# Two queues in turns begin the four copies of v in self-attention

## The chip, the cores and the metric

The kernel runs on one core of a Trainium2 chip. The metric is the device time of one launch in microseconds, and what counts is the median of several runs. All data are float32. The engines are named as the profile names them: PE multiplies matrices (PEld is its weight load), DVE and ACT work on vectors and scalars, POOL is the third vector engine. SP computes nothing; its queue begins DMA transfers and waits for what they need. ACT's queue can begin transfers too, between its own computing instructions.

## What is computed

The reference is one decoder layer on x of shape 2 x 1024 x 256, in three parts, each closed by a residual sum and a layer normalisation. Only the first part is touched:

```python
q, k, v = split_heads(x @ Wq), split_heads(x @ Wk), split_heads(x @ Wv)   # 16 heads of 64
q, k = apply_rope(q), apply_rope(k)
sim = einsum('bid,bjd->bij', q, k) * scale          # causal
attn = softmax(sim)
out = einsum('bij,bjd->bid', attn, v) @ Wo + bo
```

After it come cross-attention to 77 context rows and a feed-forward block that only the better half of the tokens, chosen by a router, goes through.

## The kernel before

Self-attention is done for 16 pairs of heads: 8 pairs for each of the two batch entries, numbered 0 to 15. A pair goes through named steps, and one list of steps per period (`steps`, L487), with an opening (L526) and an ending (L539) written out by hand, puts the steps of several pairs into one order. That order is the order of instructions on every engine's queue: nothing is reordered later, and each queue takes its instructions one after the other. An instruction that has to wait holds up all that stand behind it on its own queue, and nothing on the others.

The steps that matter here, with their letters in the lists:

- `P`, `E`: PE projects x to k, q and v (L268, L303); ACT copies the results out of PSUM (L276, L312).
- `d`: SP begins two transfers that swap neighbouring rows of k and q, `turned<-raw`. `s` and `a`: POOL multiplies them by the sine table (L291) and adds them (L295), which finishes the rotary embedding. Both are done for two halves of the tokens, numbered 0 and 1.
- `S`: PE makes scores (L342). `T`: DVE masks them and finds the least (L355). `X`: ACT takes exponentials (L363). `R`: DVE transposes them within blocks of 32 by 32 into `p_t` (L372).
- `w`: SP writes v to a buffer in device memory, `v_d<-v`. `l`: the four copies `v<-v_d`, the subject of this change. DVE's transposes leave each group of 32 keys on its own quarter of the 128 partitions, and the output matmuls may multiply any quarter with any group of keys; so each quarter needs all of v: 512 KB in each of four copies, every one of them to 32 partitions.
- `V`: PE multiplies v with the exponentials (L410), eight steps V0 to V7. The first four matmuls of V0 each read another quarter. `O`: ACT copies the four results out (L422); in the last pair DVE does it (L428).
- `D`, `B`, `M`: the sums' reciprocals go to memory and come back spread along partitions (`inv_d`, `over`), and POOL scales the output by them (L431). `W`: SP stores the output, `attn_d<-out_pair`.
- `A`, `C`, `Y`, `Z` close a tile of 128 tokens of the first batch entry: SP loads the outputs of all its pairs (`attnT<-attn_d`), PE projects them (L473), the rest normalises. `f`, `F`, `g`, `z` do so for the second.

There is one v4 buffer. The copies for a pair may therefore begin only when V7 of the pair before has ended, and they must have landed before V0 of their own pair. In the lists `l` stands behind the first `O` steps of the pair before. Those wait for the end of V7 on ACT anyway, so that ACT hardly waits once more when it comes to the copies.

On SP's queue each period has, in this order: `d0`, `B`, `w`, `d1`, `D`, the three weight loads of `L`, `W`, `A`. In the ending the order differs: around the copies of pair 15 the list reads `14O3 5C 15R10 15l 15X21 13M 15T30 ... 14O1 13W 15S4 14Q ... 6A 6C`. There `13W` (attn_d) and `6A` (attnT for tile 6) stand behind `15l` in the list but on another queue, and PE runs `6C` before `15V0`. In that place `1=` stands for a few matmuls that nobody reads.

## Time and profile before

| what | value |
|---|---|
| median of 3 runs | 831.27 us (830.59 to 837.27) |
| profiled execution | 842.25 us |
| its span, first to last instruction | 840.5 us |
| granted PE clock, mean | 0.985 |
| ACT queue, all 64 copies of v, issue time | 309 / 443 / 1402 ns min / median / max |

The profile is of one execution. A line of the timeline gives the start, the busy time, engine, source line, operation, what is written and read, the count, and in brackets how long the engine had been idle and what ended that. `SPq` and `ACTq` are the queues that begin transfers; the duration of such a line is the time of issuing, not of moving the data. A transfer's landing is told separately, as the time from issue until its completion is seen. A line of sums over a window gives the stretch, its length, the busy time and count of PE, PEld, DVE, ACT and POOL, the granted clock, the mean busy share of the 16 DMA engines, and GB/s. Pair numbers are not in the profile; they come from counting the copies.

### The profile page before, as it was taken

What the parts mean: (1) busy time and instruction counts of PE and PEld (TensorE: products, weight loads), DVE (VectorE), ACT (ScalarE), POOL (GpSimd) and SP (SyncE); (2) the same over time, 40 slices, a digit from 0 to 9 for tenths busy, and PEclk for the clock granted to TensorE, in tenths of its full rate; (3) what the DMA queues carried; (4) which work ended last, traced back from release to release, by engine and by line L of the source; (5) the groups of instructions that cost most, each with busy time, mean ns of one, the idle gap of its engine ahead of it and who ended that gap; (6) DMA issues with size and microseconds to landing.
All of it is one profiled execution on the core that took longest, in us unless ns stands there. A gap on an engine that the chain in (4) does not pass through costs nothing.

```text
span 840.5 us, 26580 instructions
## 1 busy us (share of the span) xinstructions
PE 796.4 (95%) x11432; PEld 629.2 (75%) x11432; DVE 581.4 (69%) x1345; ACT 356.6 (42%) x842; POOL 367.6 (44%) x261
## 2 busy tenths in 40 slices
PE   8999999999999899999999989899999999998996
PEld 4566688888788787788787867589778888876655
DVE  2558679668668568668776796535477788876673
ACT  2545455556456455554544554200443332333220
POOL 2733554555454554463661653213032222261574
PEclk9999999999999999999999999899999999999999
DMA  5445387577468467567474585564360000011131
GB/s 176 140 135 138 117 216 181 180 197 195 128 168 205 149 187 184 172 170 183 161 195 130 150 208 161 130 188 151 132 210 1 1 1 0 1 51 51 51 101 50
DMA packets 65328, 112.32 MB, mean 134 GB/s; under 512 B 6497, under 2 KB 43707, under 8 KB 65211
## 3 DMA queue, kind: packets, MB, share of 16 engines
q1 hardware_dynamic: 54459, 72.87, 26.9%
q10 hardware_dynamic: 9216, 33.56, 18.6%
q0 software_dynamic: 1536, 4.20, 1.3%
q8 instruction: 90, 1.47, 0.8%
q14 instruction: 27, 0.22, 0.1%
HBM read 71.24 MB, written 22.59 MB: 112 GB/s over the span
## 4 chain that ended last, share of the span: by engine, by line
PE 79%; DVE 10%; issue 4%; POOL 4%; DMA 1%; ACT 1%; POOLq 0%; SPq 0%; DVEq 0%; ACTq 0%
PE po_self L410 17%; PE ps_scores L342 16%; PE pp_kq L268 13%; PE pp_v L303 7%; PE po_proj L473 5%; PE ps_cross L945 5%; PE po_cross L997 4%; DVE reach L800 2%; PE pp_h L888 2%; PE po_ffn L899 2%; DVE pT L372 2%; PE unread L244 1%; PE pt_p L977 1%; POOL e L966 1%; POOL comp L830 1%
## 5 line engine op out<-in xcount | busy, mean ns | idle before, releaser
L355 DVE CUSTOM_DVE_ANT_0 p<-ps_scores,fence 128x512 f32<-128x512 f32 (+7 forms) x256 | 179.7, 751 | 127.2 <-PE ps_scores L342 126.8
L363 ACT ACTIVATE p<-p,neg 128x768 f32<-128x768 f32 (+7 forms) x256 | 196.3, 768 | 162.5 <-DVE neg L355 160.6
L410 PE MATMUL po_self<-pT,v 32*64 32x256 f32 (+6 forms) x7808 | 160.4, 298 | 22.3 <-issue 17.5
L372 DVE STREAM_TRANSPOSE pT<-p 128x768 f32<-128x768 f32 (+7 forms) x256 | 175.8, 740 | 3.4 <-ACT p L363 1.8
L410 PEld LDWEIGHTS po_self<-pT,v 32*64 32x64 f32 x7808 | 139.1, 133 | 47.6 <-issue 36.3
L342 PE MATMUL ps_scores<-kq 64*128 64x256 f32 (+3 forms) x1056 | 151.8, 420 | 2.9 <-issue 1.3
L342 PEld LDWEIGHTS ps_scores<-kq 64*128 64x128 f32 x1056 | 95.0, 191 | 45.2 <-issue 29.8
L291 POOL TENSOR_TENSOR turned<-turned,sin 128x1024 f32<-128x1024 f32 x31 | 73.1, 2360 | 109.7 <-DMA turned<-raw 105.0
L268 PE MATMUL pp_kq<-xT,w_pair 128*128 128x256 f32 (+2 forms) x516 | 118.8, 382 | 1.3 <-ACT xT L203 0.8
L288 POOL TENSOR_TENSOR kq<-raw,cos 128x1024 f32<-128x1024 f32 x31 | 73.3, 2363 | 103.8 <-ACT raw L276 103.8
L268 PEld LDWEIGHTS pp_kq<-xT,w_pair 128*128 128x128 f32 x516 | 87.1, 191 | 25.2 <-issue 11.3
L966 POOL TENSOR_TENSOR e<-e,inv 128x616 f32<-128x616 f32 x32 | 38.2, 1215 | 113.8 <-DVE inv L965 96.1
L120 POOL TENSOR_TENSOR rs<-ve,neg_half 128x1 f32<-128x1 f32 x48 | 27.6, 577 | 113.3 <-DVE ve L118 112.1
L295 POOL TENSOR_TENSOR kq<-kq,turned 128x1024 f32<-128x1024 f32 x31 | 73.4, 2369 | 1.4
L997 PE MATMUL po_cross<-packed,pT 128*128 128x256 f32 (+1 forms) x320 | 72.5, 381 | 0.0
L945 PE MATMUL ps_cross<-wqk,x1T 128*128 128x308 f32 x256 | 69.2, 423 | 0.0
L997 PEld LDWEIGHTS po_cross<-packed,pT 128*128 128x128 f32 (+1 forms) x320 | 60.7, 192 | 8.9
L303 PEld LDWEIGHTS pp_v<-w_pair,xT 128*128 128x128 f32 x512 | 61.1, 192 | 4.0 <-issue 2.2
L303 PE MATMUL pp_v<-w_pair,xT 128*128 128x128 f32 x512 | 62.2, 275 | 0.0
L945 PEld LDWEIGHTS ps_cross<-wqk,x1T 128*128 128x128 f32 x256 | 47.4, 190 | 16.2 <-issue 0.7
L958 ACT ACTIVATE e<-e 128x616 f32<-128x616 f32 x32 | 22.9, 717 | 83.0 <-DVE e L954 83.0
L473 PE MATMUL po_proj<-wo,attnT 128*128 128x256 f32 x224 | 51.6, 381 | 1.5 <-ACT out_pair L422 1.0
(128 smaller groups left out, 830.7 us busy)
## 6 DMA issues: line engine op xcount, KB each, us to landing
v<-v_d ACTq DMA_DIRECT2D x64, 512.0 KB, 8.4
turned<-raw SPq DMA_DIRECT2D x64, 256.0 KB, 4.5
v_d<-v SPq DMA_DIRECT2D x16, 512.0 KB, 4.6
over<-inv_d SPq DMA_DIRECT2D x32, 256.0 KB, 4.7
attn_d<-out_pair SPq DMA_DIRECT2D x14, 512.0 KB, 3.8
attnT<-attn_d SPq DMA_DIRECT2D x8, 512.0 KB, 5.4
vo_d<-vo SPq DMA_DIRECT2D x2, 1232.0 KB
attnT<-attn_d SPq DMA_DIRECT2D x3, 768.0 KB, 6.5
```

The lines of the kernel that those rows point to most:

```text
L268: TE.matmul(pp[:, cols], self.w[:, c, "kq".index(of), :], x_ts[self.b, n][:, c, cols], start=(c == 0), stop=(c == NC - 1),)
L288: E.tensor_tensor(self.kq[:, :, n * NB : (n + 1) * NB], self.raw[n], self.twice(cos, n), ALU.mult)
L295: E.tensor_tensor(dst, dst, self.turned[n], ALU.add)
L303: TE.matmul(pv[:, i, :], x_ts[self.b, 2 * n // NT][:, c, toks], self.w[:, c, 2, :], start=(c == 0), stop=(c == NC - 1),)
L342: TE.matmul(self.ps[j][:, cols], self.kq[rows, 1, t * P : (t + 1) * P], self.kq[rows, 0, cols.start - at : cols.stop - at], start=True, st ...
L355: V.tensor_tensor_reduce(p[:, span], self.ps[j][:, span], fence[:, T - (t + 1) * P :], -SCALE, -MASKED, ALU.add, ALU.min, neg[:, i : i + 1],)
L363: A.activation(p[:, span], p[:, span], AF.Exp, bias=neg[:, i : i + 1], scale=-1.0, accum_out=self.sums[:, j, t : t + 1],)
L372: V.transpose(p_t[:, first : first + t * step + 1 : step, :], self.p[g, j][:, span].rearrange("p (n k) -> p n k", k=P),)
L410: ins = TE.matmul(self.po[r][j * D : (j + 1) * D, n:, :], self.v4[rows, NT * k + n, j * D : (j + 1) * D], p_t[rows, first:last:step, k * R ...
L473: TE.matmul(self.po, of, wo[:, c, :], start=(c == 0), stop=(c == NP - 1))
L945: TE.matmul(ps[:, g, : Q * S], self.x_t[:, c, :], wqk[:, c, self.b, h : h + Q, :].rearrange("p h s -> p (h s)"), start=(c == 0), stop=(c = ...
L997: TE.matmul(po, self.p_t[:w, k, :], packed[self.b][:w, k, :], start=(k == 0), stop=(k == NK - 1))
```

## The change

In step `l` the four copies are no longer all begun by ACT: quarters 0 and 2 stay on ACT's queue, quarters 1 and 3 go to SP's. Sizes, sources, destinations and the place in the lists stay.

```diff
                 self.v4 = s1.tile([P, K4, P], F32, tag="v4", name="v4")
                 for r in range(4):
-                    nc.scalar.dma_start(
+                    (nc.scalar, nc.sync)[r % 2].dma_start(
                         self.v4[r * R32 : (r + 1) * R32, :, :].rearrange("k (c n) d -> k c (n d)", c=4),
                         self.v_d.rearrange("c k e -> k c e"),
                     )
```

In the built program ACT has 32 copies fewer and SP 32 more; PE, DVE and POOL keep their instructions in the same order. On SP the two copies of a pair stand right behind the store of the next pair's v (`v_d<-v`), and for pairs 1 to 15 the first of them waits for PE. In most pairs the next transfer behind them is `turned<-raw`. In pair 14 it is `attn_d<-out_pair`; in pair 15 `over<-inv_d` stands ahead of them, and behind them come `attn_d<-out_pair` and two loads `attnT<-attn_d`.

## The prediction

> **What bounds the kernel now.** I read the page first: busy times, the chain that ended last, the table of DMA issues. Then, for the stage the change touches (self-attention, about 57 to 554 us), the timeline of every engine, sums over windows, and the landing times of single transfers.

> ```profile
> span 840.5 us, 26580 instructions
> PE 796.4 (95%) x11432; PEld 629.2 (75%) x11432; DVE 581.4 (69%) x1345; ACT 356.6 (42%) x842; POOL 367.6 (44%) x261
> PE 79%; DVE 10%; issue 4%; POOL 4%; DMA 1%; ACT 1%; POOLq 0%; SPq 0%; DVEq 0%; ACTq 0%
> v<-v_d ACTq DMA_DIRECT2D x64, 512.0 KB, 8.4
> turned<-raw SPq DMA_DIRECT2D x64, 256.0 KB, 4.5
> ```

> PE is the bound: 95% busy, 79% of the chain. The 64 copies are 4 for each of 16 pairs of heads. DMA holds 1% of the chain and ACT 1%, so a cheaper issue or an earlier landing pays only where PE waits for it. Two places decide: an ordinary pair, and the last one.

> An ordinary pair (number 3; POOL, SP and PE of the timeline, then two window sums, whose last two columns are the DMA share and GB/s):

> ```profile
> 139.76 1.13 SPq L219 DMA_DIRECT2D turned<-raw  x2
> 148.72 2.36 POOL L291 TENSOR_TENSOR turned<-turned,sin 128x1024 f32<-128x1024 f32 x1 [4.24 <-DMA turned<-raw]
> 151.16 2.38 POOL L295 TENSOR_TENSOR kq<-kq,turned 128x1024 f32<-128x1024 f32 x1
> 153.79 0.49 PE L342 MATMUL ps_scores<-kq 64*128 64x256 f32 x2
> ...
> 133.00:145.00 12.00, 12.00 (x176) 10.73 (x158) 10.63 (x17) 7.53 (x15) 4.81 (x3) 1.00 0.84 178
> 145.00:149.00 4.00, 4.00 (x29) 3.62 (x30) 2.10 (x2) 1.71 (x5) 0.28 (x1) 1.00 1.03 330
> ```

> ACT issues the four copies from 134.24 to 136.32. The last lands 11.8 us after its issue, at 147.6, and the first matmul that reads them starts at 150.36: 2.8 us to spare. The turned halves that SP issues at 139.76 land only at 148.0. The sine step waits for them, the sum ends at 153.54, and the scores start at 153.79 with PE never idle. So what stands close to PE is turned, not v, with 0.25 us of slack here.

> The last pair (15; SP, ACT, then PE):

> ```profile
> 515.18 0.33 SPq L219 DMA_DIRECT2D attn_d<-out_pair  x1
> 515.55 3.61 SPq L219 DMA_DIRECT2D attnT<-attn_d  x2
> ...
> 519.36 3.78 ACTq L322 DMA_DIRECT2D v<-v_d  x4
> 523.25 0.94 ACT L363 ACTIVATE p<-p,neg 128x768 f32<-128x768 f32 x1 [3.73 <-DVE neg L355]
> ...
> 527.55 3.72 PE L473 MATMUL po_proj<-wo,attnT 128*128 128x256 f32 x16 [0.96 <-ACT out_pair L422]
> 533.03 0.81 PE L410 MATMUL po_self<-pT,v 32*64 32x256 f32 x4
> 535.44 0.61 PE L410 MATMUL po_self<-pT,v 32*64 32x256 f32 x2 [1.60 <-DMA v<-v_d]
> 537.52 1.08 PE L410 MATMUL po_self<-pT,v 32*64 32x256 f32 x9 [1.47 <-DVE x L121]
> ```

> Here PE does wait for v: quarters 2 and 3 land at 535.3 and 537.4, and the matmuls start at 535.44 and 537.52. (The second wait is put down to DVE, but the landing is 0.1 us before it.) SP has already sent this stage's other transfers, at 515.18 and 515.55, before ACT begins.

> **The change, part by part.**

> *ACT loses two of four issues.* 64 issues take 32.1 us of ACT's queue, so 32 of them give back 16 us, 1 us a pair. ACT waits 160.6 us for DVE's minima alone, which covers it: in ordinary pairs the next exponential starts when DVE releases it. Where PE waits for ACT's copies out of PSUM the trace shows 0.48 us (492.14) and 0.96 us (527.55). I take 0.2 us of gain; the bounds are 0 and 0.5, since the second wait is replaced below.

> *SP gains two issues, about 0.5 us each, and a wait.* They stand behind the store of v and wait for the last matmul that reads the old v4 (the end of V7). Queued behind are the next turned halves, inv_d, the weights, attn_d and attnT. In pairs 1 to 13 SP is idle after that store until the turned halves, whose source comes 4 us or more after V7's end (134.1, then 139.76): cost nothing. The cover is that gap; without it each pair would pay up to 1 us on turned. Pair 0 waits for no matmul. In pair 14 the row of attn_d is issued at 489.75 and V7 ends at 489.94: nothing.

> *Do the copies land earlier?* They begin at most 0.15 us earlier (SP need not finish ACT's copy out of PSUM first). The four move 2.1 MB; a window wholly inside, 522 to 533, moved 208 GB/s with the DMA share at 1.00. [...] If the limit were the queue, the near row would be 330 GB/s (145 to 149) and the copies 10.1 - 6.4 = 3.7 us shorter. I take 0: DMA already shows a share of 1.00 on one queue's copies. Even 3.7 us is worth nothing in ordinary pairs, where PE doesn't wait.

> *Do the turned halves land later, now behind two copies on their own queue?* [...] behind SP's own copies they would land at 148, 2 us later, and with 0.25 to 2.4 us of slack in pairs 2 to 9 PE would pay 8.3 us in all (1.17, 1.75, 1.41, 1.0, 0, 1.58, 0, 1.42). The row disagrees: they already land at 148.0, after the last copy at 147.6. They already queue behind all four copies, whichever queue those use. I take 0, with 8.3 at the far end.

> *The last pair changes order.* This is the one term that isn't hidden. In the built program SP's two copies of pair 15 stand ahead of attn_d and attnT, and must wait for V7 of pair 14, which ends at 519.12. So attnT is issued not at 515.55 but after two copies and attn_d, at about 520.6, and its data go out behind the copies on the same queue. The matmuls at 527.55 (L473) need it, and PE takes them before pair 15's output. When does it land? Pair 14 shows nearly the same heap in another order: attn_d issued at 489.75, four copies, the turned halves (0.52 MB), attnT landing at 506.9, 17.15 us in all. Without the turned halves (0.52 MB at 330 GB/s, 1.6 us) it is 15.55 us from 519.2: 534.7. Then PE: L473 starts 7.15 us later; from it to the first output matmul was 533.03 - 527.55 = 5.48 us, so output starts at 540.2. By then v has long landed (519.2 + 13.4 = 532.6, as from 134.24 to 147.6). Before, output really ran from 537.52 with 6 matmuls done (0.2 us), as if from 537.3. Loss: 2.9 us. Everything from there to 600 is PE back to back (its idle sums to about 1 us), so it reaches the end.

> Sum: 2.9 - 0.2 = 2.7 us on the profiled 842.25 (span 840.5 and 1.75 around it), 844.95. That execution is 1.3% above the median of the runs, so 831.27 x 844.95 / 842.25 = 833.9 us.

> **The rivals.**

> *A: the last pair gains.* If only SP's own two copies go ahead of attn_d and attnT, and ACT's two share the rest of the time, then from 520.3 it is 1.05 MB at 209 GB/s (5.0 us) and 1.05 MB at 330 (3.2 us): attnT lands at 528.5, output starts at 534.0, 3.3 us sooner, and with ACT's 0.2 us the time is 827.8. For it: v's late landing costs PE 3.7 us now. Against it: the turned halves of pair 3, which queue behind all four copies.

> *B: slower, by the turned halves.* One mechanism: two copies ahead of them on SP's queue make them 2 us later in every pair; it decides as soon as the delay exceeds 0.25 us. 8.3 + 2.7 = 11 us: 842.2. [...] Against it: 148.0 after 147.6.

> *C: it does nothing.* The order on SP costs nothing since attnT and v trade places evenly: 831.3.

> **How the numbers follow.** Forecast 0.6 (832 to 836.5), A 0.15 (827 to 830), B 0.13 (837 to 845), C 0.12 (830 to 832). The range 829.5 to 839 leaves out about half of A and over half of B, and some scatter of the runs (830.59 to 837.27). What a measurement of this kernel tells from no change is about 1%, 8.3 us: only B's upper part is beyond it. Faster 0.02, same 0.87, slower 0.11.

> **What the profile after would show.** Ordinary pairs: ACT's copies x2 a pair, turned landing within 0.5 us of 8.2 after issue, scores without PE idle before them. Last pair: attn_d at 520 rather than 515.18; before L473 a wait of 6 to 8 us for attnT; output running without waits for v. Wrong if PE idles before L342 in most pairs (B), or if L473 near 527 isn't late (A).

## The result, and the profile after

The changed kernel takes 841.63 us (median of 17 runs, 836.6 to 849.09) against 837.1 us for the kernel before (17 runs beside them, 830.59 to 844.79). The ratio is 1.0071, interval 1.0049 to 1.0093: about 5.9 us slower (4.1 to 7.8); the two medians differ by 4.5 us. The forecast was 833.9 us in a range that ended at 839.0; direction and place were right, the size was not. The ratios leave out runs more than 1.5% above the fastest of their kernel, and as every kernel here scatters by about as much, the medians of all runs are given beside a ratio where the two differ.

Two things went wrong. The base: 831.27 us was the median of three runs; 17 runs of the same kernel, those three among them, have a median of 837.1, and 59, 36 and 54 others 837.45, 838.51 and 837.04. And the effect: 5.9 us instead of 2.7.

The two profiled executions hide all that: 842.25 us before, 841.96 after (its span is in the page), because PE reached the end of V7 of pair 14 at 519.12 before and at 513.45 after. That stretch scatters by some 9 us from run to run (511.5 to 520.2 in the fourteen traces of this study), with no instruction on PE changed. From V7's end on, the traces can be compared.

The page after (first the span; then the shares of the chain that ended last; then DMA issues, with the median from issue to landing):

```profile
span 840.2 us, 26598 instructions
PE 80%; DVE 8%; issue 4%; POOL 4%; DMA 3%; ACT 1%; SPq 0%; POOLq 0%; DVEq 0%; ACTq 0%
turned<-raw SPq DMA_DIRECT2D x64, 256.0 KB, 4.2
v<-v_d ACTq DMA_DIRECT2D x32, 512.0 KB, 7.7
v<-v_d SPq DMA_DIRECT2D x32, 512.0 KB, 10.4
```

DMA's share of the chain went from 1% to 3%. The turned halves land no later than before (median 4.2 us, before 4.5). That they land 2 us later in each pair was an estimate of rival B, which no trace showed.

Ordinary pair 3 of the kernel after, from the timeline:

```profile
140.63 1.14 SPq L219 DMA_DIRECT2D turned<-raw  x2
149.07 2.35 POOL L291 TENSOR_TENSOR turned<-turned,sin 128x1024 f32<-128x1024 f32 x1 [3.73 <-DMA turned<-raw]
151.49 2.39 POOL L295 TENSOR_TENSOR kq<-kq,turned 128x1024 f32<-128x1024 f32 x1
154.78 1.68 PE L342 MATMUL ps_scores<-kq 64*128 64x256 f32 x14
```

A stretch of the window sums of the same kernel in which only copies of v move (DMA share and GB/s last):

```profile
138.00:140.50 2.50, 2.50 (x24) 2.41 (x22) 2.50 (x5) 2.50 (x5) 0.00 (x0) 1.00 1.03 210
```

The turned halves land at 148.3, 7.7 us after their issue (before 8.2), and the scores' line carries no idle time. Copies alone move 210 GB/s; the same window of the kernel before (137.0 to 139.7) has 211. So in this pair two queues in turns neither speed the copies up nor delay what follows.

The last pair after (timeline; SP and ACT's queue, then PE):

```profile
513.48 1.73 SPq L322 DMA_DIRECT2D v<-v_d  x2
513.65 1.57 ACTq L322 DMA_DIRECT2D v<-v_d  x2
515.31 0.39 SPq L219 DMA_DIRECT2D attn_d<-out_pair  x1
515.74 11.44 SPq L219 DMA_DIRECT2D attnT<-attn_d  x2
528.25 6.14 PE L473 MATMUL po_proj<-wo,attnT 128*128 128x256 f32 x16 [7.31 <-DMA attnT<-attn_d]
536.14 6.55 PE L410 MATMUL po_self<-pT,v 32*64 32x256 f32 x268
543.56 1.79 PE L410 MATMUL po_self<-pT,v 32*64 32x128 f32 x116 [0.87 <-issue]
```

The order on SP is the one forecast: copies, then attn_d, then attnT. What the waiting copies hold up is seen in it: POOL had finished attn_d's source at 509.81, and SP issued attn_d 5.50 us later (before, 0.02 us later: 515.16 and 515.18). From 509.81 to V7's end PE, on its own queue, was busy for 3.30 of 3.64 us. (The line of 11.44 us joins two loads: the one for tile 6 is begun at 515.74, the other belongs to the second batch entry, waits for attn_d, and is begun at 526.81.) PE waits 7.31 us for attnT, and the output then runs 268 matmuls without a wait for v. One number was not forecast: the 16 matmuls of L473 take 6.14 us, and took 3.72 before. The window sums say why. They are cut at V7's end, L473, the first output matmul and the last projections, and the granted clock is the first of the last three columns. First the kernel before:

```profile
519.12:527.55 8.43, 7.47 (x33) 4.35 (x33) 8.43 (x15) 4.69 (x12) 0.00 (x0) 1.00 0.98 233
527.55:533.03 5.48, 5.48 (x21) 3.73 (x22) 5.48 (x8) 3.30 (x7) 0.00 (x0) 1.00 0.97 193
533.03:554.35 21.32, 17.41 (x509) 14.10 (x508) 5.19 (x15) 0.69 (x2) 5.62 (x6) 0.84 0.52 148
```

The same sums of the kernel after:

```profile
513.45:528.25 14.80, 7.49 (x35) 4.40 (x34) 14.49 (x22) 7.63 (x17) 0.00 (x0) 0.82 0.89 216
528.25:536.14 7.89, 7.89 (x21) 5.44 (x21) 0.75 (x1) 0.37 (x1) 0.00 (x0) 0.69 0.68 203
536.14:551.86 15.72, 13.80 (x510) 12.37 (x509) 5.90 (x14) 0.69 (x2) 5.63 (x6) 1.00 0.46 139
```

During the wait PE's granted clock fell to half (from 522.96, for 10.24 us), and it stayed there into the work behind the wait: 0.69 over the second stretch. The kernel before lost clock too, but in its third stretch (0.84): its half clock began at 536.2, behind the first and in the second of its two waits for v, and lasted 6.83 us.

### The profile page after: what moved, and what is told of

It is laid out like the page before. It is cut to its first block, busy times and chain, and to the rows that moved or that the text cites. A ratio compares the mean times of both kernels' runs of the same rounds, so it can differ in the third digit from the quotient of the medians.

```text
span 840.2 us, 26598 instructions
## 1 busy us (share of the span) xinstructions
PE 794.4 (95%) x11432; PEld 628.0 (75%) x11432; DVE 581.1 (69%) x1345; ACT 356.7 (42%) x842; POOL 367.7 (44%) x261
## 3 DMA queue, kind: packets, MB, share of 16 engines
q8 instruction: 90, 1.47, 0.8%
## 4 chain that ended last, share of the span: by engine, by line
PE 80%; DVE 8%; issue 4%; POOL 4%; DMA 3%; ACT 1%; SPq 0%; POOLq 0%; DVEq 0%; ACTq 0%
PE po_self L410 17%; PE ps_scores L342 16%; PE pp_kq L268 13%; PE pp_v L303 7%; PE po_proj L473 6%; PE ps_cross L945 5%; PE po_cross L997 4%; DVE reach L800 2%; PE pp_h L888 2%; PE po_ffn L899 2%; PE unread L244 2%; POOL comp L830 2%; DMA attnT<-attn_d 1%; PE pt_p L977 1%; POOL e L966 1%
## 5 line engine op out<-in xcount | busy, mean ns | idle before, releaser
L363 ACT ACTIVATE p<-p,neg 128x768 f32<-128x768 f32 (+7 forms) x256 | 196.3, 768 | 169.7 <-DVE neg L355 165.8
L355 DVE CUSTOM_DVE_ANT_0 p<-ps_scores,fence 128x512 f32<-128x512 f32 (+7 forms) x256 | 179.7, 751 | 123.3 <-PE ps_scores L342 123.0
L410 PE MATMUL po_self<-pT,v 32*64 32x256 f32 (+6 forms) x7808 | 155.6, 294 | 17.1 <-issue 15.3
L410 PEld LDWEIGHTS po_self<-pT,v 32*64 32x64 f32 x7808 | 136.6, 130 | 40.1 <-issue 32.7
L342 PE MATMUL ps_scores<-kq 64*128 64x256 f32 (+3 forms) x1056 | 150.2, 417 | 2.0 <-issue 1.3
L342 PEld LDWEIGHTS ps_scores<-kq 64*128 64x128 f32 x1056 | 93.7, 190 | 44.0 <-issue 29.4
L291 POOL TENSOR_TENSOR turned<-turned,sin 128x1024 f32<-128x1024 f32 x31 | 73.2, 2360 | 106.1 <-DMA turned<-raw 106.0
L295 POOL TENSOR_TENSOR kq<-kq,turned 128x1024 f32<-128x1024 f32 x31 | 73.5, 2370 | 1.4
L473 PE MATMUL po_proj<-wo,attnT 128*128 128x256 f32 x224 | 54.1, 394 | 8.4 <-DMA attnT<-attn_d 7.3
## 6 DMA issues: line engine op xcount, KB each, us to landing
turned<-raw SPq DMA_DIRECT2D x64, 256.0 KB, 4.2
v<-v_d ACTq DMA_DIRECT2D x32, 512.0 KB, 7.7
v<-v_d SPq DMA_DIRECT2D x32, 512.0 KB, 10.4
v_d<-v SPq DMA_DIRECT2D x16, 512.0 KB, 4.8
over<-inv_d SPq DMA_DIRECT2D x32, 256.0 KB, 4.4
attn_d<-out_pair SPq DMA_DIRECT2D x14, 512.0 KB, 3.8
attnT<-attn_d SPq DMA_DIRECT2D x8, 512.0 KB, 5.2
```

The lines of the kernel that those rows point to most:

```text
L295: E.tensor_tensor(dst, dst, self.turned[n], ALU.add)
L342: TE.matmul(self.ps[j][:, cols], self.kq[rows, 1, t * P : (t + 1) * P], self.kq[rows, 0, cols.start - at : cols.stop - at], start=True, st ...
L355: V.tensor_tensor_reduce(p[:, span], self.ps[j][:, span], fence[:, T - (t + 1) * P :], -SCALE, -MASKED, ALU.add, ALU.min, neg[:, i : i + 1],)
L363: A.activation(p[:, span], p[:, span], AF.Exp, bias=neg[:, i : i + 1], scale=-1.0, accum_out=self.sums[:, j, t : t + 1],)
L410: ins = TE.matmul(self.po[r][j * D : (j + 1) * D, n:, :], self.v4[rows, NT * k + n, j * D : (j + 1) * D], p_t[rows, first:last:step, k * R ...
L473: TE.matmul(self.po, of, wo[:, c, :], start=(c == 0), stop=(c == NP - 1))
```

## The experiments

The theory, called T: the loss is made in the last pair, where SP's two copies stand ahead of attn_d and attnT. The rival, B as in the prediction: every pair pays a little. A second question came from the profile: is the half clock a part of the loss, or chance?

This table, cut as the windows above, is used throughout (us; from each kernel's trace). The first three begin the last pair's copies on ACT, the next four put SP's two ahead of attnT; the means used below are of three rows each, without e1_halves.

| kernel | V7 of pair 14 to L473 | L473 to first output | first output to last projections | sum |
|---|---|---|---|---|
| before | 8.44 | 5.48 | 21.32 | 35.24 |
| before, again | 8.02 | 5.72 | 20.19 | 33.93 |
| e1_last_act | 8.13 | 5.48 | 19.84 | 33.45 |
| after | 14.79 | 7.90 | 15.72 | 38.40 |
| after, again | 14.70 | 8.36 | 18.72 | 41.77 |
| e1_only_last | 14.71 | 7.70 | 17.91 | 40.32 |
| e1_halves | 14.46 | 7.27 | 17.32 | 39.05 |
| e1_early_load | 7.32 | 6.13 | 19.39 | 32.84 |
| e2_halves_early | 7.32 | 6.16 | 18.89 | 32.36 |
| e2_before_early | 8.96 | 5.44 | 16.42 | 30.82 |
| e2_keep_busy | 21.05 | 5.38 | 17.34 | 43.76 |
| e3_keep_busy | 14.83 | 5.45 | 24.33 | 44.61 |
| e3_late_sp | 7.49 | 6.15 | 17.40 | 31.04 |
| e3_late_sp_halves | 7.32 | 5.88 | 16.82 | 30.02 |

### The last pair undone, and the last pair alone

```diff
-                    (nc.scalar, nc.sync)[r % 2].dma_start(
+                    (nc.scalar if self.n == 15 else (nc.scalar, nc.sync)[r % 2]).dma_start(   # e1_last_act
+                    ((nc.scalar, nc.sync)[r % 2] if self.n == 15 else nc.scalar).dma_start(   # e1_only_last
```

> The changed kernel, with the four copies of pair 15 alone begun by ACT again; pairs 0 to 14 keep two queues. Theory T (the loss is made in the last pair, where SP's two copies stand ahead of attn_d and attnT): the last pair is as in the kernel before, attn_d is issued before the copies, L473 waits about 1 us, and the ratio to the kernel before is 0.998 to 1.002. Rival B (every pair pays a little, by turned or by the two queues): 15 of 16 pairs still pay, the ratio stays at 1.005 to 1.007.

> The kernel before, with the copies of pair 15 alone begun by two queues. Theory T: the whole loss is here, ratio 1.005 to 1.009, with L473 waiting about 7 us for attnT in the last pair. Rival B: one pair of 16 pays, ratio 1.000 to 1.001.

Measured: e1_last_act 835.99 us (22 runs) against 837.45 (59 runs), ratio 1.0002 (0.9976 to 1.0029). e1_only_last 844.66 us (6 runs), ratio 1.0128 (1.0067 to 1.0189). The timeline of e1_last_act:

```profile
513.56 3.47 ACTq L322 DMA_DIRECT2D v<-v_d  x4
521.45 3.72 PE L473 MATMUL po_proj<-wo,attnT 128*128 128x256 f32 x16 [0.65 <-ACT out_pair L422]
528.45 0.61 PE L410 MATMUL po_self<-pT,v 32*64 32x256 f32 x2 [0.88 <-DMA v<-v_d]
530.61 7.75 PE L410 MATMUL po_self<-pT,v 32*64 32x256 f32 x262 [1.55 <-DMA v<-v_d]
```

The timeline of e1_only_last:

```profile
515.14 11.65 SPq L219 DMA_DIRECT2D attnT<-attn_d  x2
527.89 5.94 PE L473 MATMUL po_proj<-wo,attnT 128*128 128x256 f32 x16 [6.95 <-DMA attnT<-attn_d]
```

Fifteen pairs with two queues cost nothing that the interval (0.3% either way) can show; the last pair alone costs as much as all sixteen or more. In e1_last_act PE waits for ACT and v, as before; in e1_only_last for attnT, as after. T holds and B falls. The interval of e1_only_last reaches above T's 1.009, with six runs.

### The load of attnT moved ahead of the copies

```diff
-            15X00 14V1 13B 14V2 ... 15X41 15X40 6A 6C
+            15X00 14V1 13B 6A 14V2 ... 15X41 15X40 6C
```

> The changed kernel, with the load of attnT for tile 6 moved in the ending's list from just ahead of its projection to just behind the step 13B, so that SP begins it before the last pair's two copies. Theory T: L473 no longer waits for a load behind the copies, v has landed about 13 us after V7 of pair 14, and the stretch from V7's end to the last output matmuls is 5 to 9 us shorter than in the changed kernel; ratio to the kernel before 0.993 to 0.998. Rival B: the loss of the other pairs stays, 1.003 or more.

Measured: 838.5 us (22 runs), ratio 1.0032 (1.0002 to 1.0062). That is below the changed kernel's 1.0071, but not below 1 as expected. The timeline:

```profile
527.50 3.62 PE L473 MATMUL po_proj<-wo,attnT 128*128 128x256 f32 x16
535.54 6.38 PE L410 MATMUL po_self<-pT,v 32*64 32x256 f32 x262 [1.05 <-DVE inv L384]
542.09 0.55 SPq L219 DMA_DIRECT2D attnT<-attn_d  x1
546.47 3.72 PE L473 MATMUL po_proj<-wo,attnT 128*128 128x256 f32 x16 [1.61 <-DMA attnT<-attn_d]
```

The wait before L473 is gone and PE no longer waits for v. What is late next shows twice: the reciprocals (inv, 1.05 us) and the load for tile 7, begun only at 542.09 behind the reciprocals' round trip, for which PE waits 1.61 us. By the table the stretch is 5.6 us shorter than in the changed kernel, but only 1.4 us shorter than the mean of the first three rows (34.2); my expectation had taken the gain from the wrong base. Why the runs are 0.3% above the kernel before rather than 0.2% below stays open; its profiled execution came late to the last pair (V7's end at 520.18), within what V7's end scatters.

### Both halves of the partitions at one time

```diff
-                    (nc.scalar, nc.sync)[r % 2].dma_start(
+                    (nc.scalar, nc.sync)[r // 2].dma_start(
```

> The changed kernel, with quarters 0 and 1 on ACT's queue and 2 and 3 on SP's, so that the two queues write to both halves of the partitions at one time, instead of quarters 0 and 1 together and then 2 and 3. If the partitions' side limits the copies [...]: the rate while only copies run rises from about 208 GB/s towards 330, the copies of a pair land 3 to 5 us sooner, and the last pair's wait for attnT shrinks from 7.3 us to about 3; ratio to before 1.001 to 1.004. If the queue or the memory side limits them: rate and landings as in the changed kernel, ratio 1.005 to 1.009.

Measured: 841.48 us (22 runs), ratio 1.0049 (1.0021 to 1.0077). Its window sums in pair 3, first copies alone, then copies with the turned halves (DMA share and GB/s last):

```profile
136.00:138.50 2.50, 2.50 (x24) 2.44 (x22) 2.50 (x4) 2.50 (x5) 0.00 (x0) 1.00 1.06 283
139.00:144.00 5.00, 5.00 (x32) 4.17 (x29) 4.96 (x8) 3.30 (x6) 4.37 (x2) 1.00 0.96 310
```

Its last pair, from the timeline:

```profile
525.98 5.52 PE L473 MATMUL po_proj<-wo,attnT 128*128 128x256 f32 x16 [6.70 <-DMA attnT<-attn_d]
```

The copies run at 283 GB/s instead of 210, and in pairs whose last copies are seen to land they end about 11 us after the first issue instead of 13 (pair 13: 10.8 against 13.7). All four copies read the same `v_d`, and the two forms differ only in which quarters stand side by side on the two queues, so it is the partitions' side that held the copies to 210 GB/s here. By what mechanism is not shown. PE doesn't wait for v in pair 3 (its output matmuls start at 149.39 without a wait), and the gain is worth nothing there. In the last pair it failed: the wait shrank from 7.31 to 6.70 us only, not to about 3. The packet records show the two queues there sharing unevenly (from 515 to 517 us ACT's moves 197 to 225 GB/s and SP's almost nothing), so that the two halves are not written side by side throughout. Why is not shown. The ratio lies just below the second forecast and above the first, and does not tell it from the changed kernel's.

### The wait filled, so that PE isn't idle

```diff
-            15X40 6A 6C 1=
+            15X40 6A 4= 4= 4= 4= 6C 1=      # e2_keep_busy
+            15X40 6A 4= 4= 6C 1=            # e3_keep_busy
```

> The changed kernel itself once more, so that it is timed and profiled beside the next ones. The last pair's wait for attnT again 6.5 to 7.5 us, ratio to before 1.004 to 1.009. If the clock is a second part of the loss, the granted clock is halved again near the first projection after this wait, and the mean clock of its runs is 0.001 to 0.003 lower than that of the kernel before; if not, the half clock of the first profile was chance and is absent here.

> The changed kernel with 16 more matmuls that nobody reads, put on PE between the sums of pair 14 and the projection that waits for attnT; the wait is filled for some us, the load lands no sooner. Clock theory: PE does not idle long enough, the granted clock stays whole, the 16 matmuls of L473 take 3.7 us instead of 6.1, and the ratio to before is 1.002 to 1.005. If the half clock is chance or follows something else: as the changed kernel, 1.006 to 1.009.

> The changed kernel with 16 unread matmuls (6.95 us by the run with 32, which took 13.9) between the sums of pair 14 and the projection that waits for attnT, so that they end about when the load lands. Clock theory: the wait of 7.2 us shrinks to under 1, no half clock follows, the 16 matmuls of L473 take 3.6 us instead of 6.1 to 6.6, and L473 starts at the same 14.7 us after V7 of pair 14; ratio to before 1.002 to 1.005. If the half clock is chance: 1.006 to 1.010.

Measured: the changed kernel again 847.22 us (7 runs) against 838.51 (36 runs), ratio 1.0095 (1.0058 to 1.0132). The ratio is just above the expected range, and the mean clock over all runs is 0.980 against 0.987, a larger distance than expected. The half clock is there again, from 528.5 for 10.24 us; timeline of this second profile:

```profile
532.82 6.60 PE L473 MATMUL po_proj<-wo,attnT 128*128 128x256 f32 x16 [7.22 <-DMA attnT<-attn_d]
```

e2_keep_busy turned out to hold 32 unread matmuls rather than the 16 of its expectation, 13.9 us of work, so L473 came 6.3 us later than in the changed kernel: 849.38 us (6 runs), ratio 1.0158 (1.0113 to 1.0202). It can't answer for the time, but it does for the clock: no half clock anywhere in the last pair, and L473 takes 3.62 us. e3_keep_busy holds 16. The timeline of e2_keep_busy (first line), then of e3_keep_busy:

```profile
535.58 3.62 PE L473 MATMUL po_proj<-wo,attnT 128*128 128x256 f32 x16
...
521.11 7.03 PE L244 MATMUL unread<-ident 128*128 128x512 f32 x16
528.62 3.69 PE L473 MATMUL po_proj<-wo,attnT 128*128 128x256 f32 x16 [0.47 <-DMA attnT<-attn_d]
549.50 0.58 PE L410 MATMUL po_self<-pT,v 32*64 32x96 f32 x4 [4.99 <-issue]
550.02 6.22 PE L473 MATMUL po_proj<-wo,attnT 128*128 128x256 f32 x16
```

In e3_keep_busy L473 starts 14.83 us after V7, as in the changed kernel (14.79 and 14.70), and takes 3.69 us instead of 6.14 and 6.60. So the half clock there was caused by the idle wait, and it cost about 2.5 us (5.45 instead of 7.9 to 8.4 in the table's second column). But the kernel did not win them: 846.55 us (22 runs) against 837.04 (54 runs), a ratio of 1.0114 by the medians of all runs, and of 1.0041 (1.001 to 1.0071) when 11 of the 22 are left out. The second lies within the clock theory's forecast, the first does not, so the forecast for the time is not confirmed. In the profiled execution PE waits 4.99 us until 549.50 for no engine and no data ("issue"), and a half clock of 6.83 us begins during that wait. Why the waits for issue grow when the long wait is filled is open; what they are is told at the end.

### The loads moved forward, with and without the change

Both tiles' loads go ahead of what held them, once on two queues by halves (e2_halves_early), once with all copies on ACT (e2_before_early):

```diff
-            13B 14V2 ... 15X40 6A 6C ... 0f 1f 1= 15V0 14D 4Z 14B 6Y 15V1 15V2 15V3 7A 15V4
+            13B 6A 14V2 ... 15X40 6C ... 0f 1f 7A 1= 15V0 14D 4Z 14B 6Y 15V1 15V2 15V3 15V4
```

> The changed kernel with quarters 0 and 1 on ACT's queue and 2 and 3 on SP's, and with the loads of attnT for tile 6 (from ahead of its projection to behind 13B) and tile 7 (from behind 15V3 to behind 1f) moved forward. Theory T: neither projection waits for a load, v lands before the output wants it; the stretch from V7 of pair 14 to the last projections is 4 to 6 us shorter than in the changed kernel, ratio to before 0.995 to 0.999. Rival: another wait takes their place (the sums' reciprocals), ratio 1.000 to 1.004.

> The kernel before (all four copies on ACT) with the same two loads moved forward. Theory T: these loads did not wait here, so nothing is gained, 0.998 to 1.002; v still lands late, with two waits of about 1 to 1.5 us before output matmuls. If moving the loads is what helps by itself: 0.995 to 0.998.

Measured: e2_halves_early 838.82 us (14 runs), ratio 1.0000 (0.9966 to 1.0035), so the rival's lower end: PE waits no more for loads or v, but 1.05 us for inv and 2.98 us in all for issue. e2_before_early 836.83 us (22 runs), ratio 0.9982 (0.9961 to 1.0003), not distinguishable from the kernel before. The timeline of e2_before_early:

```profile
531.19 0.89 PE L410 MATMUL po_self<-pT,v 32*64 32x256 f32 x6
533.10 6.07 PE L410 MATMUL po_self<-pT,v 32*64 32x256 f32 x262 [1.02 <-DVE inv L384]
```

Here the expectation failed: PE waits for inv but not for v, with all four copies on ACT, and by the table the stretch is 3.4 us shorter than the mean of the first three rows. So two queues are not needed for v to come in time. In this execution V7 ended 3.2 us after attn_d had landed, against 0.3 us in the first profile, so that the load behind attn_d was done before most of the copies moved; whether the moved loads or that chance did it is not shown. A stretch that is shorter in one profile need not show in the runs: by the table e2_halves_early gains 1.8 us on that mean, and its ratio is 1.

### Two queues, with SP's copies behind the load for tile 6

ACT's two copies of the last pair stay; SP's become a step `k`, right behind 6A. All pairs use two queues.

```diff
+            def part(self, rows):
+                for r in rows:
+                    (nc.scalar, nc.sync)[r % 2].dma_start(        # r // 2 in e3_late_sp_halves
...
-            15X40 6A 6C
+            15X40 6A 15k 6C
```

> The changed kernel, with SP's two copies of pair 15 begun behind attn_d and the load of attnT for tile 6 (a step of their own just behind 6A); ACT's two stay. All pairs use two queues. Theory T (only the order on SP in the last pair costs): L473 waits about 1 us as in the kernel before, v lands as late as there (about 18 us after V7), ratio 0.998 to 1.002. Rival B (using two queues costs by itself): 1.005 or more.

> As the last one, but with quarters 0 and 1 on ACT's queue and 2 and 3 on SP's in every pair. With the copies of ordinary pairs landing 2 us sooner in this form (11 against 13 us) the last pair's v lands 2 to 4 us sooner than in the kernel before, and its two waits for v of about 1.5 us go: ratio 0.995 to 0.999. If those waits are replaced by the reciprocals' (inv): 0.998 to 1.001.

Measured: e3_late_sp 835.48 us (22 runs) against 837.04 (54 runs), ratio 0.9973 (0.9949 to 0.9997). e3_late_sp_halves 834.17 us (17 runs), ratio 0.9937 (0.9902 to 0.9971); by the medians of all runs 0.9966. The timeline of e3_late_sp (SP's first two lines), then of e3_late_sp_halves (in both the lines of PE and of the copies stand 3 lower in the code):

```profile
514.33 1.47 SPq L219 DMA_DIRECT2D attnT<-attn_d  x1
517.59 0.80 SPq L325 DMA_DIRECT2D v<-v_d  x2
...
523.06 3.62 PE L476 MATMUL po_proj<-wo,attnT 128*128 128x256 f32 x16
528.94 0.89 PE L413 MATMUL po_self<-pT,v 32*64 32x256 f32 x6
530.85 6.07 PE L413 MATMUL po_self<-pT,v 32*64 32x256 f32 x262 [1.02 <-DVE inv L387]
538.16 1.79 PE L413 MATMUL po_self<-pT,v 32*64 32x128 f32 x116 [1.24 <-issue]
```

No wait for attnT, none for v; the reciprocals' 1.02 us are late next. e3_late_sp reads the same (0.93 us for inv), so v came sooner than expected there: the last landing seen is 13.9 us after V7's end, not about 18. In e3_late_sp, with the same 32 copies on SP and the same wait on SP, only the place of two of them behind the load for tile 6 differs from the changed kernel, and the loss is gone. e3_late_sp_halves is faster than both kernels: by 0.3 to 0.6% than before, and, by dividing the two ratios, by 1.0 to 1.3% than after (0.9966 and 0.9937 over 1.0071). Both did a little better than expected. How much of it is the halves and how much the order is not shown: the intervals of the two kernels overlap.

### The kernel before, once more

> The kernel before once more, for its trace. The tail as in the first profile: L473 waits about 1 us, output matmuls wait for v twice. If the half clock after these waits is chance, its place differs from the first profile (536.2, 6.83 us); if it follows the waits, it is again within 5 us of them.

Measured: 838.35 us in one run. The timeline:

```profile
524.10 3.72 PE L473 MATMUL po_proj<-wo,attnT 128*128 128x256 f32 x16 [0.26 <-ACT out_pair L422]
532.92 7.75 PE L410 MATMUL po_self<-pT,v 32*64 32x256 f32 x262 [1.28 <-DVE ve L118]
```

The waits are smaller than in the first profile (0.26 and 1.28 us, and 0.47 for v at 531.03), and a half clock of 3.41 us begins at 534.2, 1.2 us after the last of them ended: it follows the waits, in this profile as in the first.

## Why the prediction was wrong

*ACT's two issues fewer (0.2 us) and SP's two more (nothing in ordinary pairs).* Nothing contradicts either: e1_last_act, which has both in 15 pairs, is at 1.0002. 0.2 us is below what its interval of 0.3% can show.

*The copies land no earlier, the turned halves no later (0 and 0).* Right: 210 against 211 GB/s in the window with copies alone, landings 7.7 against 8.2 us after issue in pair 3, no idle before the scores, and 1.0002 for fifteen pairs so made. But a DMA share of 1.00 was no reason for it: the share was 1.03 at 210 GB/s, and in e1_halves 1.06 at 283. The price of rival B, 8.3 us, which rested on its estimate of 2 us a pair, is excluded.

*The last pair, 2.9 us.* The place and the chain were right, and the sum was mis-sized. Means of the table's rows with copies on ACT (34.2 us) and with SP ahead (40.2) differ by 6.0 us, as much as the measured loss of 5.9. (By the medians of all runs that loss is 4.5, and the two other measurements of this order, 1.0095 and 1.0128, lie higher, with 7 and 6 runs.) Against the forecast, term by term:

- L473 starts later: forecast 7.15 us, measured 6.5 (14.73 against 8.20). Near enough.
- "From it to the first output matmul was 5.48 us", carried over unchanged: this is the step that failed. It takes 7.99 us instead of 5.56, 2.4 us more, because PE's clock is halved behind a wait of 7 us. e3_keep_busy shows it by taking the idleness away: there it takes 5.45.
- The output no longer waits for v: forecast a credit of 4.3 us (from 533.03 to 537.3), measured 3.0 (17.45 against 20.45). The waits for v did go, 2.4 us of them on average. But waits for issue grew from 0.8 to 2.7 us on average, and PE was busy 2.4 us less, 1.7 of it because less half clock fell into this stretch. So this credit was 1.3 us too large. With three profiles of each and this scatter, that split stays a reading, not a proof.

6.5 + 2.4 - 3.0 = 5.9, against 7.15 - 4.3 = 2.9.

Part of the half clock moved rather than came. The clock lost (length times one minus the granted clock) is 2.6 us in the second stretch and 0.6 in the third with SP ahead, 0 and 2.3 with the copies on ACT: 0.9 us more in all. The prediction counted neither.

One line of the kernel before was also read too quickly: "SP has already sent this stage's other transfers, at 515.18 and 515.55". The second line joins two loads, and the second of them began at 518.79, landed at 533.33 and moved beside the copies. That fits v's late landing there, 18.3 us after V7's end, against 13.9 in e3_late_sp, where that load stands behind SP's two copies.

*The base.* "831.27 x 844.95 / 842.25" took the median of three runs for the kernel's time and called the profiled execution 1.3% high. The later runs show that those three lay low by about 6 us; the profiled execution was only 0.6% above the later medians. Of the miss of 7.7 us (841.63 against 833.9), 5.8 come from here, and 1.9 from the effect, taken by the medians (4.5 against 2.6).

*Rival A* (attnT lands at 528.5, by queues that share) had L473 start no later than 9.4 us after V7; it started after 14.7 us. *Rival C* is excluded by the interval.

## What to carry to other kernels

When a transfer is moved to another queue, read in the built order what stands behind it there, at the ends of the loop too: here fifteen of sixteen places cost nothing that shows (ratio 1.0002), and one where a load that PE needs next stood behind two waiting copies cost 0.7%. Put the waiting transfers behind the ones that are ready. A long idle stretch of PE can cost more than its length, since the work behind it can start at half clock (here the granted clock was 0.69 over the 7.89 us behind a wait of 7.31, which cost 2.4 us); and scatter of 1% in the runs means that three runs are no base for a forecast.

## What the runs showed of the hardware

*Waits for issue.* The trace lists DMA queues of their own for instructions; in the kernel after one of them has 90 packets, all of 16 KB. The fourteen traces hold 213 waits of PE of over 0.5 us, before 560 us, that are put down to "issue", and every one ends 2.2 to 3.1 us after such a packet starts. Most packets have no such wait behind them: 906 of 1119 between 15 and 560 us. But those behind the others add up to 14 to 23 us of a trace, up to 4.99 us in one place, and differ from run to run. That PE waits for these packets is read from the times alone; what makes one start late was not tested.
